# Edge-gated graph layer with residual layer norm: the first 16 parts' edges in one tile, head work queued behind table chunks, two more gather buffers, other batch sizes at the end

## The chip, the cores and the metric

The kernel runs on one core of a Trainium2 chip. A core has five engines that run their own instruction streams and wait for each other through semaphores: TensorE (PE, matrix products and transposes; PEld is its weight load), VectorE (DVE), ScalarE (ACT, activations and copies), GpSimd (POOL, which here only issues gathers) and SyncE (SP, which here issues transfers). The metric is device time in microseconds from start to end of one execution; lower is better.

## The reference

There are N = 12500 nodes with 128 features and E = 412500 directed edges (200000 edges in both directions and one loop for each node), sorted by destination.

```
theta = x[dst] - x[src]
w     = sigmoid(relu(theta @ W1 + b1) @ W2 + b2)      # one number for each edge
agg   = segment_sum(w * theta, dst)
indeg = segment_sum(1, dst)
out   = layernorm(x + agg + indeg * (x @ W4 + b4))
```

Since theta is a difference, theta @ W1 is y[dst] - y[src] with y = x @ W1, and the sum of w * theta over a node's edges is x times the sum of w, less the sum of w * x[src].

## The kernel before, in words

**Parts and blocks.** The edges are cut into 403 parts of 1024 (K = 8 groups of 128; the last part has 7 groups). Two parts make a block (202 blocks). As edges are sorted by destination, the destinations of a block lie in a window of WB = 96 consecutive nodes that begins at the block's first destination, and those of a part within 41.

**Head (lines 107 to 313).** The source and destination of the first 16 parts (`FIRST = 16`) are loaded with a part to a partition, 16 partitions of 1024 numbers; `turn` (L280) converts them to float on ACT (L283) and transposes them on PE (L288), 4 groups at a time; `place_src` (L294) writes the row numbers `src_i`, which the gathers use, and `place_dst` (L300 to L312) writes destinations relative to the part (`off`) and to the window (`rel`), and notes their largest and smallest values in `bad` (a check that they fit). `base_r` is each part's first destination, 403 separate numbers (L120); from it come `base_b`, `first_c`, `base_c`, `far` and `step_c` (L231 to L251), the broadcast over partitions being a matmul (L238). Lines 137 to 204 make constants: one-hot helpers, a split of b1 in three bf16 terms, and so on. The tile framework orders the instructions of each engine; only SP's order is that of the program (`manual_schedule`, L314).

**Table.** `table_chunk` (L333) computes z = [y, x] for all nodes, 12 chunks of 1024 rows and two small ones: the rows of x come in by a transfer issued from ACT (L329), PE transposes four groups of 128 rows into the PSUM tile `pw` (L342), ACT copies them to `txT` (L344), PE multiplies by W1 into `ph` (L346); when both halves are through, DVE copies y (L348) and ACT copies x (L349) into a buffer `zt`, and SP writes it to z in HBM (L350). There are three `zt` buffers and one `pw`.

**Gathers.** `gather(s)` (L224) issues a part's K indirect transfers from POOL, each fetching 128 rows. The first NH = 8 parts fetch rows of x (so that they need not wait for z), and the later parts rows of z. There are NZ = 8 buffers `zbuf`; parts 0 to 7 take half a buffer each (zbuf 0 to 3), zbuf 4 to 6 are also the table's `zt`, and part 8 onwards goes round all of them from zbuf 4. A buffer can be filled again when its part's ACT work (L456) has read it. POOL issues in the order of the parts, and each gather waits for the landing of the one 8 before.

**Main loop (L552 to L574).** Step s issues the gather of part s + 4, the block's window (y of the 96 nodes and its spread, L360 to L386), the one-hots of part s + 2 (`one_hot`, L389), the spread of y to edges (`spread_y`, L400, PE), and `weights(s)` (L434): DVE subtracts the gathered y (L448), takes relu times W2 (L449) and sums to logits (L453); ACT makes the sigmoid (L454) and scales the gathered x rows (L456, 8 for each part). For the first 8 parts `both` (L418) computes the product with W1 on PE, as no y was gathered. `one_hot_w(s - 1)` (L409, a 128x768 compare) and `add_up(s - 2)` (L459) follow: PE sums the part's rows into the window (L474), 16 matmul instructions.

**End of a block (`total`, L487 to L524).** First up to one finished row block is stored (two in the last nine blocks), then the sums are copied (L494), PE computes x @ W4 + b4 in `pu` (L497, L498), DVE and ACT combine the terms (L505 to L509) and take mean and variance (L512, L513). The inverse root is taken for LB = 8 blocks together (L518, L519), as ACT has to switch its table between sigmoid and square root; the last three blocks close their batch at once. `store` (L480) makes `o` on DVE (L484) and SP writes it (L485); `o` has 4 buffers. At the very end the flag from `bad` is read (L580 to L586); were it set, a slow general version would run.

Of the kernel before, what the change touches and what calls it, by code (L numbers as in the profile page):

```python
# [28 lines left out]
NZ = 8  # L29
AHEAD = 4  # L30
LB = 8
NH = 8
FIRST = 16
# [4 lines left out]
def gnn_resnorm(  # L38
# [76 lines left out]


    loaded = [load(nc.sync, src, *sets[0])]
    base_r = const.tile([1, NS], I32, name="base_r")
    with nc.allow_non_contiguous_dma(reason="each part's first dst"):
        nc.sync.dma_start(  # L120
            base_r, bass.AP(tensor=dst.tensor, offset=dst.offset, ap=[[0, 1], [BE, NS]]))
    wts = const.tile([P, 2, D], F32, name="wts")
    nc.sync.dma_start(wts[:, 0, :], W1)
    loaded.append(load(nc.sync, dst, *sets[0]))
# [13 lines left out]
    nc.vector.tensor_copy(ident_b, ident)  # L138
# [10 lines left out]
    nc.vector.tensor_scalar_mul(wneg, wts[:, 0, :], -1.0)  # L149
# [7 lines left out]
    nc.scalar.activation(fix[:, :WB], iota_row[:, :WB], AF.Copy)  # L157
    nc.scalar.activation(fix[:, P:2 * P], w2_r, AF.Copy)
    iota_f = fix[:, :WB].rearrange("p (o m) -> p o m", o=1)
    w2_f = fix[:, P:2 * P].rearrange("p (o m) -> p o m", o=1)  # L160


    def at_least(name, n, v=1.0):
        c = const.tile([P, 1], F32, name=name)
        nc.vector.tensor_scalar(c, iota_p, float(n), v, op0=OP.is_ge, op1=OP.mult)
        return c

    ge = [at_least(f"ge{i}", i * SW) for i in range(4)]
    eb = [at_least(f"eb{i}", 3 * SW + i) for i in range(1, 4)]
    m12 = const.tile([P, 1], F32, name="m12")  # L170
    nc.vector.tensor_sub(m12, ge[3], ge[1])
    m2 = const.tile([P, 1], F32, name="m2")
    nc.vector.tensor_sub(m2, ge[3], ge[2])
    one_c = const.tile([P, 1], F32, name="one_c")
    nc.vector.tensor_sub(one_c, ge[3], eb[2])
    place_c = const.tile([P, 1], F32, name="place_c")
    nc.vector.tensor_add(place_c, ge[1], ge[2])
    nc.vector.tensor_scalar(place_c, place_c, -float(SW), None, op0=OP.mult)
    nc.vector.tensor_add(place_c, place_c, iota_p)
    nc.vector.scalar_tensor_tensor(place_c, ge[3], -4.0 * N, place_c, op0=OP.mult, op1=OP.add)  # L180

    YB = WB + 3
    yb_buf = [const.tile([P, D], F32, name=f"yb{i}") for i in range(2)]
    bh = const.tile([P, D], BF16, name="bh")
    b1_s = const.tile([P, D], F32, name="b1_s")
    e_c = const.tile([P, 1], F32, name="e_c")
    nc.vector.memset(b1_s, 0.0)
    for i in range(3):
        nc.vector.tensor_copy(bh, b1_r)
        nc.vector.tensor_scalar(e_c, iota_p, float(WB + i), None, op0=OP.is_equal)  # L190
        nc.vector.scalar_tensor_tensor(b1_s, bh, e_c, b1_s, op0=OP.mult, op1=OP.add)
        nc.vector.tensor_sub(b1_r, b1_r, bh)
    for t in yb_buf:
        nc.vector.tensor_copy(t[WB:, :], b1_s[WB:, :])


    behind = const.tile([P, P], F32, name="behind")
    nc.vector.memset(behind, -4.0)
    for i in range(3):
        nc.vector.tensor_copy(behind[:WB, i * SW:(i + 1) * SW], lag[:WB, :SW])  # L200
    own = behind[WB:, 3 * SW:3 * SW + 3]
    nc.vector.tensor_scalar(own, lag[WB:, 3 * SW:3 * SW + 3], float(WB - 3 * SW), 4.25,
                            op0=OP.is_equal, op1=OP.mult)
    nc.vector.tensor_scalar(own, own, -4.0, None, op0=OP.add)
# [27 lines left out]
    nc.vector.tensor_scalar(base_b, base_r[:, ::SUB], float(N - WB), None, op0=OP.min)  # L232
    base_f = const.tile([1, NS], F32, name="base_f")
    nc.vector.tensor_copy(base_f, base_r)
    first_c = const.tile([P, NS], F32, name="first_c")
    with tc.tile_pool(name="pre_ps", bufs=1, space=bass.MemoryType.PSUM) as pps:
        pb = pps.tile([P, NS], F32, name="pb")
        nc.tensor.matmul(pb, ones_r, base_f, start=True, stop=True)  # L238
        nc.vector.tensor_copy(first_c, pb)
    base_c = const.tile([P, NK, SUB], F32, name="base_c")  # L240
    for h in range(SUB):
        nc.vector.tensor_scalar(base_c[:, :, h], first_c[:, ::SUB], float(N - WB), None,
                                op0=OP.min)
    nc.vector.tensor_scalar(first_c, first_c, float(N - SW), None, op0=OP.min)
    base_cs = base_c.rearrange("p b h -> p (b h)")
    far = const.tile([P, NS], F32, name="far")
    nc.vector.tensor_sub(far, first_c, base_cs[:, :NS])
    nc.vector.memset(far[WB:, :], 0.25)
    step_c = const.tile([P, NK], F32, name="step_c")
    nc.vector.tensor_sub(step_c[:, 1:], base_c[:, 1:, 0], base_c[:, :NK - 1, 0])  # L250
# [4 lines left out]
    nc.vector.tensor_copy(bad[:, 0:1], base_c[:, 0:1, 0])  # L255
    nc.vector.tensor_scalar(bad[:, 1:2], base_c[:, NK - 1:, 0], -1.0, float(N - WB),
                            op0=OP.mult, op1=OP.add)
    nc.vector.tensor_reduce(bad[:, 2:3], step_c, AX.X, OP.max)
    nc.vector.tensor_scalar(bad[:, 2:3], bad[:, 2:3], -float(WB), None, op0=OP.add)
    nc.vector.tensor_reduce(bad[:, 3:4], step_c, AX.X, OP.min)  # L260
    nc.vector.tensor_scalar(bad[:, 3:4], bad[:, 3:4], -1.0, None, op0=OP.mult)
# [51 lines left out]

    with tc.manual_schedule(engines={SP}), tc.tile_pool(name="work", bufs=2) as wp, tc.tile_pool(  # L314
# [11 lines left out]
        def table_load(c):  # L326
            n0, np_, m = chunks[c]
            xt = tp.tile([P, TC, D], F32, name="xt", bufs=4)
            nc.scalar.dma_start(  # L329
                xt[:np_, :m, :], x[n0:n0 + np_ * m, :].rearrange("(p t) d -> p t d", t=m))  # L330
            return xt

        def table_chunk(c, xt):  # L333

            n0, np_, m = chunks[c]
            zt = zbuf[NX + c % 3]
            py = ps_h.tile([P, K, D], F32, name="ph")
            for g0 in range(0, m, G):
                g = min(G, m - g0)
                px = ps_l.tile([P, G, P], F32, name="pw")  # L340
                for j in range(g):
                    nc.tensor.transpose(px[:, j, :np_], xt[:np_, g0 + j, :], ident[:np_, :np_])  # L342
                xT = tp.tile([P, G, P], F32, name="txT")
                nc.scalar.activation(xT[:, :g, :np_], px[:, :g, :np_], AF.Copy)  # L344
                for j in range(g):
                    nc.tensor.matmul(py[:np_, g0 + j, :], xT[:, j, :np_], wts[:, 0, :],  # L346
                                     start=True, stop=True)
            nc.vector.tensor_copy(zt[:np_, :m, :D], py[:np_, :m, :])  # L348
            nc.scalar.activation(zt[:np_, :m, D:], xt[:np_, :m, :], AF.Copy)  # L349
            nc.sync.dma_start(  # L350
                z[n0:n0 + np_ * m, :].rearrange("(p t) d -> p t d", t=m), zt[:np_, :m, :])

# [56 lines left out]
        def one_hot_w(s):  # L409

            n = tiles(s)
            ow = wp.tile([P, K, WB], F32, name="ow", bufs=3)
# [46 lines left out]
        def add_up(s):  # L459
# [12 lines left out]
            end = h == SUB - 1 or s == NS - 1  # L472
            for k in range(n):
# [6 lines left out]
        def store(n):  # L480
            for _ in range(min(n, len(ready))):
                base, vb, mean, rstd = ready.pop(0)
                o = wp.tile([P, D], F32, name="o", bufs=4)
                nc.vector.tensor_scalar(o[:WB], vb, mean, rstd, op0=OP.subtract, op1=OP.mult)  # L484
                nc.sync.dma_start(out[ds(base, WB), :], o[:WB])  # L485

        def total(b):  # L487
            d = blocks.pop(b)
            pa = d["pa"]
            left = NK - 1 - b  # L490

            store(1 if left > 8 else 2)
            a = wp.tile([P, AW], F32, name="a")
            nc.scalar.activation(a[:WB], pa[:WB], AF.Copy)  # L494
            carry[0] = a
            pu = ps_l.tile([P, G, P], F32, name="pw")[:, 0, :]
            nc.tensor.matmul(pu[:WB], ones_r[:, :WB], b4_r[0:1, :], start=True, stop=False)  # L497
            nc.tensor.matmul(pu[:WB], d["xwT"][:, :WB], wts[:, 1, :], start=False, stop=True)  # L498
            if not batch:
# [4 lines left out]
            sw = wp.tile([P, 1], F32, name="sw")  # L504
            nc.scalar.activation(sw[:WB], a[:WB, D:D + 1], AF.Copy, bias=1.0)  # L505
            own = fix[:WB, (2 + b % 2) * P:(3 + b % 2) * P]
            nc.scalar.activation(own, d["xw"][:WB], AF.Copy, scale=sw[:WB])
            nc.vector.tensor_sub(v[:WB, i, :], own, a[:WB, :D])
            nc.vector.scalar_tensor_tensor(  # L509
                v[:WB, i, :], pu[:WB], a[:WB, D + 1:], v[:WB, i, :], op0=OP.mult, op1=OP.add)  # L510
# [4 lines left out]
            if len(of) == LB or left < 3:  # L515
# [7 lines left out]
            if left < 3:  # L523
                store(len(ready))  # L524
# [4 lines left out]

        fetch(0)  # L530
        fetch(1)
        xts = [table_load(0), table_load(1)]
        place_src(0, ps_l, loaded[0])
        for s in range(AHEAD):
            gather(s)
        place_dst(0, ps_l, loaded[1])
        for c in range(len(chunks)):
            if c + 2 < len(chunks):
                xts.append(table_load(c + 2))
            table_chunk(c, xts.pop(0))  # L540
# [7 lines left out]
        window(0)  # L548
        one_hot(0)
        spread_y(0)  # L550
        one_hot(1)
        for s in range(NS + 2):  # L552
# [14 lines left out]
            if s < NS:  # L567
                weights(s)
            if s + 2 < NS:
                one_hot(s + 2)  # L570
            if 0 < s <= NS:
                one_hot_w(s - 1)
# [197 lines left out]
```

## Time and profile before

| what | value |
|---|---|
| median of 3 runs | 4102.65 us (4101.36 to 4108.0) |
| the profiled execution, its time | 4108.91 us |
| its span, first to last instruction | 4107.1 us |
| busy: POOL, DVE, PE, ACT | 3053.3, 2589.6, 2435.7, 1589.9 us |
| first gather starts | 12.09 us |
| first gather from z starts | 98.77 us |
| last gather ends | 4071.37 us |
| last output store is issued | 4101.5 us |

Times in the profile's lines are microseconds from the first instruction; a timeline line gives the start, the duration, the engine (with a q where only the engine's sequencer works, as for issuing transfers), the line of the kernel, the operation, what is written and read, how many instructions stand together, and in brackets the idle time of the engine before it with what ended it. A group's line in the page gives the total busy time, the mean duration in ns, and the idle time before. "PEclk" is the share of TensorE's full clock that was granted. The profile is of one execution.

### The profile page before, as it was taken

The numbers are of one execution on the slowest core, as the hardware profiler recorded it, in microseconds if no ns is written. First come the engines' busy times: TensorE is split into PE (matmuls) and PEld (weight loads), VectorE is DVE, ScalarE is ACT, GpSimd is POOL, SyncE is SP. The second block draws the span as 40 slices with busy tenths as digits, with TensorE's granted clock in tenths as the row PEclk, the third lists the DMA queues.
The fourth block names the chain that finished last, engine by engine and source line by source line (L and its number), as shares of the span: only waits on it lengthen the run. The fifth ranks groups of instructions, "written<-read, shape, count | busy, mean of one in ns | idle before, by whom it ended". The sixth has DMA issues, their size and how long they took to land.

```text
span 4107.1 us, 52566 instructions
## 1 busy us (share of the span) xinstructions
PE 2435.7 (59%) x16083; PEld 2124.1 (52%) x16083; DVE 2589.6 (63%) x4254; ACT 1589.9 (39%) x5206; POOL 3053.3 (74%) x3232
## 2 busy tenths in 40 slices
PE   5766555565555566566556555555555555556554
PEld 4655545455445455555555555454555555545544
DVE  3587676666666666676666666666666666666665
ACT  3454344333333333343433433333334334333332
POOL 6677777777777777777777777777777777777774
PEclk8877666666766666666666666666666666666666
DMA  7333433333333333343333333333333333333332
GB/s 247 88 110 111 121 110 110 110 110 110 111 110 110 110 110 111 115 115 110 111 111 111 110 111 110 110 112 110 110 112 110 110 110 111 111 110 110 110 112 78
DMA packets 205395, 464.62 MB, mean 113 GB/s; under 512 B 59264, under 2 KB 99112, under 8 KB 203566
## 3 DMA queue, kind: packets, MB, share of 16 engines
q0 software_dynamic: 153680, 418.46, 35.7%
q1 hardware_dynamic: 49452, 36.31, 2.9%
q10 hardware_dynamic: 1970, 6.40, 0.4%
q8 instruction: 128, 2.10, 0.2%
q14 instruction: 165, 1.35, 0.1%
HBM read 438.21 MB, written 22.73 MB: 112 GB/s over the span
## 4 chain that ended last, share of the span: by engine, by line
DVE 33%; DMA 25%; PE 22%; ACT 14%; issue 5%; POOL 0%; DVEq 0%; ACTq 0%; SPq 0%; POOLq 0%
DMA zbuf<-z,src_i 24%; DVE h L448 9%; PE pa L474 9%; ACT wx L456 8%; DVE h L449 6%; DVE lg L453 5%; DVE oh L396 5%; PE pw L378 4%; DVE ow L413 3%; ACT yh L380 1%; PE ph L406 1%; ACT wx L454 1%; PE pw L368 1%; PE pd L394 1%; PE pa L470 1%
## 5 line engine op out<-in xcount | busy, mean ns | idle before, releaser
L226 POOL DMA_INDIRECT zbuf<-z,src_i x3159 | 2991.1, 947 | 988.0 <-issue 445.6
L448 DVE TENSOR_TENSOR h<-ph,zbuf 128x1024 f32<-128x1024 f32 x395 | 483.4, 1224 | 1181.7 <-DMA zbuf<-z,src_i 1181.4
L474 PE MATMUL pa<-wx,ow 128*96 128x130 f32 x6446 | 1127.9, 350 | 2.8 <-DVE ow L413 1.5
L474 PEld LDWEIGHTS pa<-wx,ow 128*96 128x96 f32 x6446 | 1092.0, 227 | 4.7 <-DVE ow L413 2.0
L456 ACT ACTIVATE wx<-zbuf,wx 128x128 f32<-128x128 f32 x3223 | 1005.0, 389 | 9.2
L394 PE MATMUL pd<-ident_b,off 128*128 128x128 bf16 x3223 | 338.4, 261 | 805.5 <-DVE oh L396 800.1
L394 PEld LDWEIGHTS <-off 128*128 128x128 bf16 x3223 | 269.9, 118 | 616.8 <-issue 604.4
L453 DVE TENSOR_REDUCE lg<-h 128x8 f32<-128x1024 f32 x403 | 486.8, 1208 | 0.2
L449 DVE SCALAR_TENSOR_TENSOR h<-h,fix 128x1024 f32<-128x1024 f32 x395 | 477.5, 1209 | 0.0
L494 ACT ACTIVATE a<-pa 96x130 f32<-96x130 f32 x202 | 55.5, 275 | 1012.9 <-PE pa L474 1012.9
L406 PE MATMUL ph<-y,oh 128*128 128x128 bf16 x3159 | 295.8, 247 | 200.9 <-DVE y L385 189.5
L413 DVE TENSOR_TENSOR ow<-fix,rel 128x768 f32<-128x768 f32 x403 | 380.6, 945 | 0.0
L406 PEld LDWEIGHTS <-oh 128*128 128x128 bf16 x3159 | 259.2, 114 | 232.5 <-issue 210.2
L396 DVE TENSOR_SCALAR oh<-pd,place_c,one_c 128x1024 bf16<-128x1024 bf16 x403 | 320.7, 796 | 42.8 <-PE ph L430 34.6
L378 PEld LDWEIGHTS pw<-yb,pick 99*128 99x128 f32 x806 | 184.3, 317 | 301.8 <-issue 224.6
L366 ACT ACTIVATE xwT<-pw 128x96 f32<-128x96 f32 x202 | 48.3, 239 | 564.0 <-PE pw L364 563.9
L378 PE MATMUL pw<-yb,pick 99*128 99x128 f32 x806 | 236.6, 447 | 39.5 <-ACT yb L370 39.3
L380 ACT ACTIVATE yh<-pw 128x256 bf16<-128x256 f32 x202 | 77.2, 382 | 428.7 <-PE pw L378 428.6
L368 PE MATMUL pw<-wts,xwT 128*96 128x128 f32 x404 | 130.2, 419 | 185.3 <-ACT xwT L366 185.0
L470 PE MATMUL pa<-a,sh 96*96 96x130 f32 x402 | 140.6, 453 | 143.1 <-DVE sh L468 141.7
L381 DVE SCALAR_TENSOR_TENSOR pw<-yh,m,pw 128x256 f32<-128x256 bf16 x202 | 98.5, 488 | 178.2 <-ACT yh L380 176.9
L364 PE MATMUL pw<-ident,xw 96*128 96x96 f32 x202 | 72.4, 359 | 207.2 <-DVE v L509 200.4
(113 smaller groups left out, 1930.1 us busy)
## 6 DMA issues: line engine op xcount, KB each, us to landing
zbuf<-z,src_i POOLq DMA_INDIRECT x3159, 2.8
z<-zbuf SPq DMA_DIRECT2D x12, 1024.0 KB
xw<-in_x_dram SPq DMA_DIRECT2D x202, 48.0 KB
out_dram<-o SPq DMA_DIRECT2D x202, 48.0 KB
xt<-in_x_dram ACTq DMA_DIRECT2D x12, 512.0 KB
zbuf<-in_x_dram,src_i POOLq DMA_INDIRECT x64, 4.2
e_i<-in_src_dram SPq DMA_DIRECT2D x2, 512.0 KB
e_i<-in_dst_dram SPq DMA_DIRECT2D x2, 512.0 KB
```

The lines of the kernel that those rows point to most:

```text
L226: nc.gpsimd.indirect_dma_start(out=rows_of(s)[:, k, :], out_offset=None, in_=z if s >= NH else x, in_offset=IndirectOffsetOnAxis(ap=src_i[ ...
L378: nc.tensor.matmul(py[:, h, :], pick[:YB], yb[:YB], start=True, stop=True)
L394: nc.tensor.transpose(pd[:, k, :], off[:, k, s:s + 1].to_broadcast([P, P]), ident_b)
L396: nc.vector.tensor_scalar(oh[:, :n, :], pd[:, :n, :], place_c, one_c, op0=OP.is_equal, op1=OP.max)
L406: nc.tensor.matmul(d["ph"][:, k, :], d["oh"][:, k, :], blocks[b]["y3"][:, h, :], start=True, stop=True)
L413: nc.vector.tensor_tensor(ow[:, :n, :], iota_f.to_broadcast([P, n, WB]), rel[:, :n, s:s + 1].to_broadcast([P, n, WB]), op=OP.is_equal)
L448: nc.vector.tensor_sub(h[:, :n, :], d["ph"][:, :n, :], zs[:, :n, :D])
L449: nc.vector.scalar_tensor_tensor(h[:, :n, :], h[:, :n, :], 0.0, w2_f.to_broadcast([P, n, D]), op0=OP.max, op1=OP.mult)
L453: nc.vector.tensor_reduce(lg[:, :n], h[:, :n, :], AX.X, OP.add)
L456: nc.scalar.activation(wx[:, k, :D], xs[:, k, :], AF.Copy, scale=wx[:, k, D:D + 1])
L470: nc.tensor.matmul(bd["pa"][:WB], sh[:WB, :WB], carry[0][:WB], start=True, stop=False)
L474: nc.tensor.matmul(bd["pa"][:WB], d["ow"][:, k, :], wx_buf[s % 3][:, k, :], start=h == 0 and k == 0 and carry[0] is None, stop=end and k = ...
```

## The change: what it does

- **First edges.** The first 16 parts' indices are loaded as one tile of 128 partitions with 128 numbers each (a partition holds one group), so that one conversion, one transpose and one copy replace two transposing rounds. Source and destination tiles have the same name in a pool with one buffer.
- **Bases in two pieces.** The first destinations of parts 0 to 15 are loaded apart from the other 387; `bases` is called for each piece, `check_bases` after the second.
- **Order at the head.** Chunks 0 and 1 of the table are written first; first bases, first destinations and constants are queued behind those chunks (`after` makes an instruction follow given ones on their engines); the long bases behind chunk 7, the first window and one-hots behind chunk 9. The table's loads use zbuf 7 and 8 instead of tiles of their own, and its transposes go into `pw` and `pd` in turn.
- **Buffers.** NZ is 10 instead of 8; `ow` has 4 buffers instead of 3; LB is 6 instead of 8.
- **Order in the loop.** `one_hot_w(s)` stands ahead of `weights(s)` (before: `one_hot_w(s - 1)` after the one-hots of s + 2). `pu` is computed ahead of the block's last sums.
- **End.** The last 12 blocks close their batch at 2 blocks, the last two at 1, and up to three blocks are stored at each of the last 12; stores come at the end of `total` instead of its beginning.

```
-NZ = 8
+NZ = 10
-LB = 8
+LB = 6
-FIRST = 16
+FIRST = P // K
...
+    def load_first(edges):
+        t = const.tile([P, P], I32, name="f_i")
+        nc.sync.dma_start(t, edges[:P * P].rearrange("(p e) -> p e", e=P))
+        return t
+    src_f = load_first(src)
...
+    load_bases(0, FIRST)
     wts = const.tile([P, 2, D], F32, name="wts")
     nc.sync.dma_start(wts[:, 0, :], W1)
-    loaded.append(load(nc.sync, dst, *sets[0]))
+    dst_f = load_first(dst)
+    load_bases(FIRST, NS)
...
+    def first_turned(t, ps):
+        f = ep.tile([P, P], F32, name="f_f")
+        nc.scalar.activation(f, t, AF.Copy)
+        pt = ps.tile([P, G, P], F32, name="pw")[:, 0, :]
+        nc.tensor.transpose(pt, f, ident)
+        return pt.rearrange("p (s k) -> p k s", k=K)
+    def place_first_src(ps):
+        nc.scalar.activation(src_i[:, :, :FIRST], first_turned(src_f, ps), AF.Copy)
...
         def table_load(c):
-            xt = tp.tile([P, TC, D], F32, name="xt", bufs=4)
+            h = c % 4
+            xt = zbuf[NX + 3 + h // 2].rearrange("p k d -> p (k d)")
...
-                px = ps_l.tile([P, G, P], F32, name="pw")
+                px = ps_l.tile([P, G, P], F32, name="pd" if g0 else "pw")
...
+            if end:
+                bd["pu"] = ps_l.tile([P, G, P], F32, name="pw")[:, 0, :]
...
-            if len(of) == LB or left < 3:
+            if len(of) == LB or (left < 12 and len(of) == 2) or left < 2:
...
-            if left < 3:
-                store(len(ready))
+            for _ in range(min(1 if left >= 12 else 3, len(ready))):
...
+        place_first_src(ps_l)
+        for s in range(AHEAD):
+            gather(s)
+        chunk()
+        chunk()
+        with after(done[0]):
+            bases(0, FIRST, ps_l)
+        with after(done[1]):
+            place_first_dst(ps_l)
+            place_c, one_c, m12, m2, yb_buf, behind = constants()
         fetch(0)
         fetch(1)
...
+        while len(done) < len(chunks):
+            chunk()
+        with after(done[7]):
+            bases(FIRST, NS, ps_l)
+            check_bases()
...
+        with after(done[9]):
+            window(0)
+            one_hot(0)
+            spread_y(0)
+            one_hot(1)
...
             if s < NS:
+                one_hot_w(s)
                 weights(s)
             if s + 2 < NS:
                 one_hot(s + 2)
-            if 0 < s <= NS:
-                one_hot_w(s - 1)
```

## The prediction

> **What bounds the kernel now.** I read the busy table first, then windows of the span, then the waits of GpSimd (POOL), then the timelines of the first 210 us and of the last 40 us.
>
> The page's busy table and one of its groups:
>
> ```profile
> PE 2435.7 (59%) x16083; PEld 2124.1 (52%) x16083; DVE 2589.6 (63%) x4254; ACT 1589.9 (39%) x5206; POOL 3053.3 (74%) x3232
> ...
> L226 POOL DMA_INDIRECT zbuf<-z,src_i x3159 | 2991.1, 947 | 988.0 <-issue 445.6
> ```
>
> No engine is full, but POOL does one thing: it issues 64 + 3159 = 3223 gathers, 947 ns each. Two equal windows (span, then PE, PEld, DVE, ACT, POOL, clock, DMA share, GB/s):
>
> ```profile
> 800.00:1600.00 800.00, 469.38 (x3088) 410.44 (x3088) 505.25 (x806) 304.88 (x1015) 605.16 (x640) 0.68 0.39 110
> 2400.00:3200.00 800.00, 465.59 (x3094) 406.15 (x3094) 509.27 (x850) 306.99 (x1019) 605.35 (x640) 0.68 0.39 111
> ```
>
> 640 gathers per 800 us in both: one per 1.25 us, 0.95 of work and 0.30 between two. DVE needs 506 of those 800 us, PE 470. So the middle is set by POOL's issue rate, and an edit there that is not on POOL moves nothing. What can move is where POOL does not issue. POOL's timeline has five such places (idle time before each, in brackets):
>
> ```profile
> 12.09 1.19 POOL L226 DMA_INDIRECT zbuf<-in_x_dram,src_i  x1 [10.33 <-ACT fix L158]
> 91.34 0.95 POOL L226 DMA_INDIRECT zbuf<-in_x_dram,src_i  x1 [0.30 <-issue]
> 98.77 0.94 POOL L226 DMA_INDIRECT zbuf<-z,src_i  x1 [6.48 <-DVE pick L375]
> 164.78 0.95 POOL L226 DMA_INDIRECT zbuf<-z,src_i  x1 [1.31 <-PE pw L378]
> 180.91 0.94 POOL L226 DMA_INDIRECT zbuf<-z,src_i  x1 [11.43 <-ACT wx L456]
> 198.36 0.94 POOL L226 DMA_INDIRECT zbuf<-z,src_i  x1 [7.76 <-ACT wx L456]
> 4070.42 0.95 POOL L226 DMA_INDIRECT zbuf<-z,src_i  x1 [0.30 <-ACT wx L456]
> ```
>
> The account: 12.09 us to the first gather; 64 gathers at 1.2485 to 92.29; 6.18 beyond the usual 0.30 until table z has landed (98.77; the releaser named, a DVE one-hot, is only what came last; the wait is for all z writes); 1.01 + 11.13 + 7.46 = 19.6 us for buffers at parts 14.5, 15 and 16; the rest at (4070.42 - 98.77 - 19.6) / 3158 = 1.2514; then 35.7 us from the last gather's end at 4071.37 to 4107.1. The buffers: parts 12 to 15 go into zbuf 0 to 3, which hold the x rows of parts 0 to 7, and ACT finished those at 187.3 (part 7) and 200.1 (part 8, zbuf 4).
>
> **The change, part by part.** Times are of the profiled execution (4108.91 us, span 4107.1).
>
> *First gather.* Before, the source indices wait for PE, where the transposes stand behind a matmul on all 403 first destinations:
>
> ```profile
> 8.89 0.26 DVE L232 TENSOR_SCALAR base_b<-base_r 1x202 int32<-1x202 int32 x1 [7.43 <-DMA base_r<-in_dst_dram]
> 9.48 1.71 PE L238 MATMUL pb<-base_f,ones_r 1*128 1x403 f32 x2 [9.48 <-DVE base_f L234]
> 11.58 0.23 ACT L294 ACTIVATE src_i<-pw 128x64 int32<-128x64 f32 x1 [5.97 <-PE pw L288]
> ```
>
> After, one tile, one transpose and one copy come first on PE. But on ACT the order is: copy of the indices (from 3.46, after the table load; 128x128, about 0.28), the issue of table load 2 (it waits for W1), the copy of chunk 0 (1.04), the issue of load 3 (it waits for load 1), and only then src_i. Loads 0 and 1, 1 MB, had arrived by 6.0 in the trace's packets; W1 should land around 6, no longer behind 403 four-byte packets. So src_i ends near 7.1, gather 0 starts at 7.5 (6 to 10). With 64 x 1.2485, POOL is ready for z at 87.4.
>
> *Table.* Its order on PE, ACT and DVE now puts chunks 0 and 1 ahead of destinations and constants. The dst tile uses the same buffer as the src tile and is issued last on SP, behind the long base list (landed at 8.87 before; say 9.5), so it lands near 12; ACT holds its copy ahead of chunk 0's first txT. So: txT 12.3, matmuls at half clock to 16.3, copy 1.22, z write 0 at 17.8 (29.3 before) and 1 at 21.5. Then DVE has about 40 small operations (first bases, checks, constants; some 8 us by their durations before) ahead of chunk 2's copy, and four `ow` (0.94 each) and two `sh` before chunk 5's: writes 2, 3, 4 near 30.4, 33.8, 36.8. Write 2 stood at 38.7 before, so it is two chunks ahead. Seven full chunks and two small ones remain. Compute: one half-chunk at full and at half clock:
>
> ```profile
> 59.66 1.06 PE L342 MATMUL pw<-ident,xt 128*128 128x128 f32 x4
> 61.47 2.07 PE L346 MATMUL ph<-wts,txT 128*128 128x128 f32 x8 [0.75 <-ACT txT L344]
> 65.14 1.16 PE L346 MATMUL ph<-wts,txT 128*128 128x128 f32 x8 [0.75 <-ACT txT L344]
> 66.13 0.60 PE L342 MATMUL pw<-ident,xt 128*128 128x128 f32 x4
> ```
>
> A chunk is 2 x (0.60 + 1.16) = 3.5 us or 2 x (1.06 + 2.07) = 6.3; the second PSUM buffer (pw, pd in turn) removes the 0.75 waits, which made it 4.7 and 7.35 before. The Trainium skill ("TensorE: Matmul & The Clock Gate", Part 1) says an idle stretch of about 3.4 us halves the clock and a busy window of that length restores it. The trace has the loss (idle 39.9 to 43.75, clock 0.5 from 44.5) but not the quick return: it stayed at 0.5 until 65. By the rule seven chunks take 25 us, by the row, half of them slow, 34. Transfer: from 30 us there remain 10.8 MB of z, 3.7 MB of x and 0.052 MB/us of gathers; at 320 to 360 GB/s (the best stretches showed 311 over 20 us, 360 over 5) this takes 47 to 54 us. That is the larger: done at 77 to 84, plus the 5 us that the last landing took before: 82 to 89. POOL is ready at 87.4, so the gather from z starts at 88.0, the middle of what both leave: 10.8 us earlier. The cover is thin: each us that the table is later than 87.4 comes straight off.
>
> *Ten buffers instead of eight.* Part p's gather now needs what part p - 10 read; parts 14 to 17 use zbuf 0 to 3. With z at 88.0 and 10.0 us a part: part 17's second half asks for part 7 at 183, part 18 for part 8 at 188. The main loop starts earlier: last chunk's copy near 77 to 80 instead of 92.1, minus 3.5 us for the long bases, which DVE does just there: 12 us earlier. So parts 7 and 8 end near 175 and 188. Stall left: 0.5 of 19.6, that is -19.1 (bounds 0 and 10 left).
>
> *One-hots ahead of logits, `pu` ahead of the sums.* Same instructions, other places. DVE has 3.7 us to spare per part; nothing on the path. The smaller batches make 38 square-root groups instead of 27, with two table loads of 1.28 us in most: some 28 us of ACT, hidden in its 61% idle time.
>
> *Tail.* Before, ten stores stand at the end, each waiting for a free `o` or a semaphore:
>
> ```profile
> 4077.44 1.28 ACT L518 ACT_TABLE_LOAD   x1
> ...
> 4079.69 22.11 SPq L485 DMA_DIRECT2D out_dram<-o  x10
> ```
>
> Now four are left; the last (block 201) is bound by compute. Relative to the same last gather (landed 4073.4): DVE's order puts h of part 402 ahead of the reduction for 401, so that is 2 us of late work more: lg(401) at 4075.8 (69.2 before), wx(401) to 78.6, sum of block 200 at 79.7, then ACT switches to square root for blocks 198/199 (1.28 + 0.3), back to sigmoid (1.28 + 0.3), 0.2 + 7 wx (2.14) to 85.2, own 0.37, switch 1.28, root of 200 to 87.1; PE's last matmul waits for `pu`, which waits for v(200) on DVE, to 87.4; copy, sw, own to 88.4; four DVE operations to 89.4; root, reciprocal, o to 90.2. The last store is issued at 4090.3, not 4101.5: -11.2. Here a rule speaks against the change: "ScalarE: Activation LUTs" (What ACT_TABLE_LOAD costs) gives a switch 2.66 us with its drain. The trace has 1.28 and the next activation 0.01 later (4077.44, then 4078.73), so I take the row; by the page three switches would cost 4.1 more, leaving -7.
>
> **Sum.** -10.8 - 19.1 - 11.2 = -41.1: 4108.91 becomes 4067.8. That execution was 6.3 above the median of the runs, 4102.65, so the forecast is 4061.5 us.
>
> **Rivals.** (1) The table stays late: the DVE constants ahead of chunk 2, or a half-clock stretch, push z's landing to 97. The head gives 2 instead of 10.8: 4070. For it: two engines in one order, 0.6 us of slack. Against: even at half clock PE needs 44 us for the seven chunks and has 50. (2) The buffers' stall only moves: if the main loop starts no earlier (long bases, DVE at 95% from 200 us on), parts 7 and 8 end at 187 and 200 against 183 and 188, 12 us come back: 4074. (3) Slower: gathers themselves become dearer, by any new contention of POOL's descriptor work. Price 3223 x the added time; from 12.8 ns a gather (1%) the gain is gone, from 15.3 it is slower by 0.2%; at 30 ns the time is 4158. For it: the first two gathers took 1.19 us, beside a busy start. Against: from the 400th gather on, means over each 400 lie between 1.2510 and 1.2523 us apart, whatever stood beside them. (4) The change doesn't do what it says: gather 0 stays at 12 since src_i waits behind ACT's loads, and the tail's switches cost the page's price: 4072 to 4077.
>
> **Numbers.** 0.2% (8.2 us) is about what a measurement of this kernel can tell from no change. The sum as worked, within 10 us: 0.70; rival 1: 0.10; rival 2: 0.08; rival 4: 0.06 (all faster); no difference 0.02; rival 3: 0.04. Faster 0.94, same 0.02, slower 0.04. Range: table (5 either way), stall (to 10), tail (4), execution spread (3): 4048 to 4080.
>
> **What would show it.** First gather near 7.5, first z gather near 88; no idle time over 2 us on POOL after it; last gather ending near 4042; some 24 us from there to the end, four stores at the last. Wrong if gathers are not 1.25 us apart, if the wait before the first z gather is over 4 us, or if wx lines again release gathers around parts 17 and 18.

## The result: some seven tenths of the gain that was forecast

| | kernel before | changed kernel |
|---|---|---|
| median of 6 runs | 4106.1 us (4101.36 to 4109.25) | 4076.39 us (4075.43 to 4077.38) |
| profiled execution, its span | 4108.91, 4107.06 us | 4076.45, 4074.68 us |

The ratio is 0.9929 (95% interval 0.9916 to 0.9942). The forecast was 4061.5 us with a range of 4048 to 4080: the direction and the range hold, and the gain is smaller than forecast (29.7 us instead of some 41). Ratios below are to the kernel before on the same chip.

The changed kernel's page, busy table and costliest group:

```profile
PE 2401.4 (59%) x16071; PEld 2090.6 (51%) x16071; DVE 2572.8 (63%) x4264; ACT 1657.5 (41%) x5239; POOL 3056.6 (75%) x3232
...
L241 POOL DMA_INDIRECT zbuf<-z,src_i x3159 | 2994.7, 948 | 962.2 <-issue 546.2
```

Two windows of its middle and two of its end (span, then PE, PEld, DVE, ACT, POOL, clock, DMA share, GB/s):

```profile
800.00:1600.00 800.00, 458.95 (x3079) 399.87 (x3079) 498.80 (x800) 313.83 (x1014) 605.44 (x639) 0.67 0.39 110
2400.00:3200.00 800.00, 454.77 (x3080) 395.72 (x3080) 503.56 (x850) 320.21 (x1026) 605.55 (x639) 0.67 0.39 111
4047.00:4052.00 5.00, 0.00 (x0) 0.00 (x0) 2.78 (x5) 0.50 (x2) 0.03 (x1) 0.63 0.13 30
4052.00:4057.00 5.00, 4.74 (x20) 4.18 (x20) 3.23 (x7) 2.26 (x8) 0.00 (x0) 0.50 0.00 0
```

The middle is what it was, 639 gathers in 800 us. The end differs: 5 us without a matmul, then 5 us at a granted clock of 0.50. POOL's timeline (first gather, first gather from z, last gather):

```profile
10.11 1.10 POOL L241 DMA_INDIRECT zbuf<-in_x_dram,src_i  x1 [8.35 <-ACT src_i L345]
...
90.35 0.95 POOL L241 DMA_INDIRECT zbuf<-z,src_i  x1 [0.30 <-issue]
...
4046.09 0.95 POOL L241 DMA_INDIRECT zbuf<-z,src_i  x1 [0.30 <-issue]
```

After the first gather POOL never waits again: not one idle time above 0.35 us among 3222. Four terms make up the difference of the two spans, each read from the two POOL timelines. The pitch is the time from one gather's start to the next; the tail is what follows the last gather's end:

| term | forecast | measured | how |
|---|---|---|---|
| head, to the first gather from z | -10.8 | -8.4 | 98.77 to 90.35 |
| waits for buffers | -19.1 | -19.6 | all gone |
| pitch of the other 3158 gathers | 0 | +3.7 | 1.25145 to 1.25261 us |
| tail, last gather's end to the end | -11.2 | -8.0 | 35.69 to 27.65 |
| sum | -41.1 | -32.4 | |

The buffers' term is tested alone below (f3, f2). Those of the head and the tail are read from the traces: no run undoes just the edits behind them.

### The profile page after: what moved, and what is told of

It is laid out like the page before. It is cut to its first block, busy times and chain, and to the rows that moved or that the text cites. A ratio compares the mean times of both kernels' runs of the same rounds, so it can differ in the third digit from the quotient of the medians.

```text
span 4074.7 us, 52688 instructions
## 1 busy us (share of the span) xinstructions
PE 2401.4 (59%) x16071; PEld 2090.6 (51%) x16071; DVE 2572.8 (63%) x4264; ACT 1657.5 (41%) x5239; POOL 3056.6 (75%) x3232
## 4 chain that ended last, share of the span: by engine, by line
DVE 34%; DMA 22%; ACT 19%; PE 18%; issue 6%; POOL 1%; DVEq 0%; SPq 0%; ACTq 0%; POOLq 0%
DMA zbuf<-z,src_i 21%; ACT wx L515 13%; DVE h L507 9%; PE pa L539 8%; DVE lg L512 8%; DVE h L508 7%; DVE oh L455 5%; ACT wx L513 2%; PE pw L437 2%; DVE pw L440 2%; PE ph L465 1%; PE pd L453 1%; PE pw L427 1%; PE pa L529 1%; POOL zbuf L241 1%
## 5 line engine op out<-in xcount | busy, mean ns | idle before, releaser
L539 PEld LDWEIGHTS pa<-wx,ow 128*96 128x96 f32 x6446 | 1075.3, 222 | 17.6 <-ACT wx L515 15.2
L515 ACT ACTIVATE wx<-zbuf,wx 128x128 f32<-128x128 f32 x3223 | 985.6, 388 | 11.0
L465 PE MATMUL ph<-y,oh 128*128 128x128 bf16 x3159 | 313.9, 246 | 231.2 <-DVE y L444 172.7
L423 PEld LDWEIGHTS pw<-ident,xw 96*128 96x128 f32 x202 | 32.6, 162 | 602.2 <-DVE v L560 596.8
L442 ACT ACTIVATE ym<-pw 128x256 bf16<-128x256 f32 x202 | 76.6, 379 | 421.1 <-DVE pw L440 421.1
L513 ACT ACTIVATE wx<-lg,b_c 128x8 f32<-128x8 f32 x403 | 123.3, 306 | 245.2 <-DVE lg L512 244.7
```

The lines of the kernel that those rows point to most:

```text
L465: nc.tensor.matmul(d["ph"][:, k, :], d["oh"][:, k, :], blocks[b]["y3"][:, h, :], start=True, stop=True)
L513: nc.scalar.activation(wx[:, :n, D], lg[:, :n], AF.Sigmoid, bias=b2_c)
L515: nc.scalar.activation(wx[:, k, :D], xs[:, k, :], AF.Copy, scale=wx[:, k, D:D + 1])
L539: nc.tensor.matmul(bd["pa"][:WB], d["ow"][:, k, :], wx_buf[s % 3][:, k, :], start=h == 0 and k == 0 and carry[0] is None, stop=end and k = ...
```

## Experiments

There are twelve runs of nine kernels, from three chips, and the chip decides what each can tell. The f runs are from a chip like that of the profiles (kernel before 4109.9 us). The e and the g runs are from two other chips, on each of which the kernel before takes 5141 us (5140.82 and 5140.66): there TensorE holds up the loop, and they answer a question that had not been asked. They are told last.

### Buffers without the head (f3), head without the buffers (f2)

f3 is the kernel before with the ten buffers; the table's loads go into zbuf 7 and 8, as there is no room for tiles of their own beside ten buffers.

```
-NZ = 8
+NZ = 10
...
-            xt = tp.tile([P, TC, D], F32, name="xt", bufs=4)
+            h = c % 4
+            xt = zbuf[NX + 3 + h // 2].rearrange("p k d -> p (k d)")
...
```

> The kernel before with the ten buffers alone, on a chip whose kernel before takes about 4103 us. Theory: 19.6 us of waits for buffers fall to about 1.3 us, first gather 12.1, first gather from z 98.8, tail 35.7: 18 us faster, 4088. Rival, the stall only moves: 7 us faster, 4099.

Measured: 4086.25 us (4083.95 to 4092.25), ratio 0.9950 (0.9933 to 0.9967). POOL's timeline, first gather, first from z, and the first of part 15 (which had waited 11.43 us):

```profile
11.89 1.20 POOL L226 DMA_INDIRECT zbuf<-in_x_dram,src_i  x1 [10.12 <-ACT fix L158]
...
96.02 0.94 POOL L226 DMA_INDIRECT zbuf<-z,src_i  x1 [3.92 <-DMA e_i<-in_src_dram]
...
166.02 0.95 POOL L226 DMA_INDIRECT zbuf<-z,src_i  x1 [0.30 <-ACT txT L429]
```

No wait is left at parts 14 to 18: 19.6 us gone, and the wait for z is 2.6 us shorter in this execution, so the span falls by 22.5 us (4107.06 to 4084.55). The rival "the stall only moves" falls.

f2 undoes the same in the changed kernel (NZ = 8, `xt` of their own).

> The changed kernel with NZ = 8 again and the table's loads in tiles of their own, on a chip whose kernel before takes about 4103 us. Theory: the earlier head already shrinks the stall; part 15 asks at 160.4 for part 6 (ACT until 164.3) and part 16 at 175 for part 8 (182.2): 12 us come back, 4088. If buffers and head simply add: 19.6 us come back, 4096. If the earlier main loop alone would have removed the stall: 4076.

Measured: 4086.33 us (4084.82 to 4089.30), ratio 0.9948 (0.9932 to 0.9965). POOL's timeline, the three places where it waits:

```profile
164.84 0.94 POOL L241 DMA_INDIRECT zbuf<-z,src_i  x1 [4.49 <-ACT wx L514]
...
170.29 0.94 POOL L241 DMA_INDIRECT zbuf<-z,src_i  x1 [0.75 <-PE pa L538]
...
182.62 0.95 POOL L241 DMA_INDIRECT zbuf<-z,src_i  x1 [7.64 <-ACT wx L514]
```

Beyond the usual 0.30 these are 12.0 us, where the theory had 12 (in the changed kernel ACT is through with part 6 at 164.3 and with part 8 at 182.2). The span is 10.25 us longer than the changed kernel's, as pitch and tail came out 2 us shorter in this execution; the medians differ by 9.9. In waits of POOL, buffers are worth 19.6 us with the old head and 12.0 with the new one. The new head lets the main loop run some 17 us earlier (part 7 done at 169.7 instead of 187.3) and so takes 7.6 of the stall away itself. The gains of the two edits overlap; only measured together, or with the times at which each buffer comes free, do they add to the right sum.

### Where the head's missing 2.4 us are (f1)

ACT's timeline in the changed kernel from the landing of the indices to the first gather's release (ACTq lines are the issuing of the table's loads):

```profile
5.22 0.31 ACT L339 ACTIVATE f_f<-f_i 128x128 f32<-128x128 int32 x1 [2.28 <-DMA f_i<-in_src_dram]
...
8.22 0.33 ACTq L379 DMA_DIRECT2D zbuf<-in_x_dram  x1
8.60 1.06 ACT L399 ACTIVATE zbuf<-zbuf 128x1024 f32<-128x1024 f32 x1 [3.07 <-DMA b_r<-in_L_gnn_b_dram]
...
9.56 0.27 ACT L345 ACTIVATE src_i<-pw 128x128 int32<-128x128 f32 x1
```

PE had the transposed indices ready at 6.13. ACT, in order, held their last copy until 9.56 behind a load's issue, which waited until 8.22, and a chunk's copy. f1 moves both conversions to DVE; it also makes the one-hot `pick` by another instruction, which is read elsewhere (the pitch).

```
-        nc.scalar.activation(f, t, AF.Copy)
+        nc.vector.tensor_copy(f, t)
...
-        nc.scalar.activation(src_i[:, :, :FIRST], first_turned(src_f, ps), AF.Copy)
+        nc.vector.tensor_copy(src_i[:, :, :FIRST], first_turned(src_f, ps))
...
-                nc.vector.tensor_scalar(pick[:YB], behind[:YB],
-                                        far[:YB, b * SUB + h:b * SUB + h + 1], None,
-                                        op0=OP.is_equal)
+                nc.vector.tensor_tensor(pick[:YB], behind[:YB],
+                                        far[:YB, j:j + 1].to_broadcast([YB, P]),
+                                        op=OP.is_equal)
```

> The changed kernel with two edits that are read at different places. (a) The conversion and the placing of the first 16 parts' indices go to DVE, which is idle there, in place of ACT, which issues a load and copies a chunk between the two: theory, first gather at 6.8 instead of 10.1 us, still no wait before the first gather from z (the table was complete at about 79, POOL asks at 87), so 3.3 us; rival, the table is delayed and POOL waits for it at 87: nothing. (b) The one-hot pick by a tensor_tensor compare: theory, gathers of over 975 ns go, mean pitch from the 400th gather on 1.2527 to 1.2510, 5 us; rival, they stay, 0 us. Both theories: 4068; both rivals: 4076.

Measured: 4076.36 us (4075.76 to 4083.85), ratio 0.9923 (0.9906 to 0.9939). The timeline of its head, and POOL's first gather from z:

```profile
5.20 0.23 DVE L339 CAST f_f<-f_i 128x128 f32<-128x128 int32 x1 [4.02 <-DMA f_i<-in_src_dram]
...
6.06 0.29 DVE L345 CAST src_i<-pw 128x128 int32<-128x128 f32 x1 [0.63 <-PE pw L341]
...
6.64 1.10 POOL L241 DMA_INDIRECT zbuf<-in_x_dram,src_i  x1 [4.88 <-DVE src_i L345]
...
87.78 0.94 POOL L241 DMA_INDIRECT zbuf<-z,src_i  x1 [0.30 <-issue]
```

The trace agrees with part (a): the first gather at 6.64 (6.8 expected), no wait at 87.78. So 3.5 us before the first gather lay in ACT's queue. Of these 2.6 are left at the first gather from z, as the 64 gathers before it stand 1.268 us apart here and 1.254 in the changed kernel. In the times no gain is seen: the other three executions took 4075.76 to 4076.88 us, the changed kernel's six 4075.43 to 4077.38. They have no trace, so where the 2.6 us went is open.

Part (b) falls: the gathers above 960 ns from the 400th on are 116 here, not fewer than the changed kernel's 101. The profiled execution took 4083.85 us, and its trace shows by what: the span is 7.2 us above that of the changed kernel, 9.9 from the pitch (1.25573 us) less 2.6 of the head and 0.1 of the tail. The usual gather took 949 ns instead of 946; the traces of e2 and g4 have 949 too, the other eleven 946.

### The place of `pu` in the tail (f4)

In the changed kernel the sums of block 200 were complete 2 us later after the last gather than I had worked out, with `pu`'s matmuls among them, waiting for `v` of the block before. f4 puts `pu` behind the sums again.

```
             end = h == SUB - 1 or s == NS - 1
-            if end:
-                bd["pu"] = ps_l.tile([P, G, P], F32, name="pw")[:, 0, :]
...
             for k in range(n):
                 nc.tensor.matmul(bd["pa"][:WB], d["ow"][:, k, :], wx_buf[s % 3][:, k, :],
...
+            if end:
+                bd["pu"] = ps_l.tile([P, G, P], F32, name="pw")[:, 0, :]
```

> The changed kernel with pu computed after the block's last sums again, on a chip whose kernel before takes about 4103 us. Theory: in the tail pu ahead of the sums holds TensorE for v of the block before, 2.0 us at block 200 and 0.9 at block 201; without it the tail from the last gather's end falls from 27.7 to about 24.8 us, time 4073.5. Rival: pu then lies on the path after the last sum: tail 27.7 to 29.2, time 4076.4 to 4078.

Measured: 4074.4 us (4073.68 to 4074.8), ratio 0.9918 (0.9901 to 0.9935); but the tail is 27.95 us, not 24.8. What it gained over 4076.39 lies in the pitch (1.25194 us from the 400th gather on, against 1.2527); all its four executions are below all six of the changed kernel, which was not run beside it. The tail of 24.8 that the theory promised did not come. The changed kernel's tail: first PE's rows of an earlier block, at the full clock (`pu`, then 16 sums), then all engines from the landing of the last gather:

```profile
4039.02 0.46 PE L534 MATMUL pw<-b_r,ones_r 1*96 1x128 f32 x2
4039.41 0.46 PE L536 MATMUL pw<-wts,xwT 128*96 128x128 f32 x2
4039.70 1.94 PE L539 MATMUL pa<-wx,ow 128*96 128x130 f32 x16
...
4049.22 1.09 DVE L507 TENSOR_TENSOR h<-ph,zbuf 128x896 f32<-128x896 f32 x1 [6.51 <-DMA zbuf<-z,src_i]
...
4052.26 0.75 PE L539 MATMUL pa<-wx,ow 128*96 128x130 f32 x2 [8.01 <-ACT wx L515]
...
4052.94 0.74 PE L534 MATMUL pw<-b_r,ones_r 1*96 1x128 f32 x2
...
4054.14 3.24 PE L539 MATMUL pa<-wx,ow 128*96 128x130 f32 x14
...
4057.42 0.28 ACT L548 ACTIVATE a<-pa 96x130 f32<-96x130 f32 x1 [3.16 <-PE pa L539]
4057.71 1.28 ACT L572 ACT_TABLE_LOAD   x1
...
4059.01 0.29 ACT L572 ACTIVATE sd<-mv,eps_c 96x2 f32<-96x2 f32 x1
```

and that of f4:

```profile
4049.86 2.91 PE L533 MATMUL pa<-wx,ow 128*96 128x130 f32 x12 [7.18 <-ACT wx L515]
...
4052.70 0.74 PE L538 MATMUL pw<-b_r,ones_r 1*96 1x128 f32 x2
...
4053.37 1.18 PE L533 MATMUL pa<-wx,ow 128*96 128x130 f32 x4
...
4054.59 0.28 ACT L548 ACTIVATE a<-pa 96x130 f32<-96x130 f32 x1 [2.73 <-PE pa L533]
...
4058.74 1.28 ACT L572 ACT_TABLE_LOAD   x1
...
4060.24 2.14 ACT L515 ACTIVATE wx<-zbuf,wx 128x128 f32<-128x128 f32 x7
```

`a` comes 10.39 us after the last gather's end in the changed kernel (4057.42 less 4047.03) and 9.94 in f4 (4054.59 less 4044.65): moving `pu` gave 0.45. It is not a clean test, for the order that came out still has half of a `pu` among the sums (L538, 0.74 us). Then f4 loses the gain: the last of three table switches, with its root (1.28 + 0.3), stands ahead of the last scalings on ACT, where the changed kernel has it behind them. In both, PE had stood idle for 7 to 8 us and then ran its sums at a granted clock of 0.5 (in f4 from 4045.2 to the end): the 14 matmuls of the changed kernel take 3.24 us, 0.23 each, where 16 at the full clock took 1.94.

### The chips on which TensorE holds up the loop (e1 to e4, g1 to g4)

On these two chips TensorE pauses between matmuls for 0.5 to 2 us at a time, while it waits for nothing that the profile shows. The sums' group in the stretch 1000 to 2000 us, first the changed kernel of the profiles above, then the same kernel on the third chip (g1):

```profile
L539 PE MATMUL pa<-wx,ow 128*96 128x130 f32 x1600 | 281.4, 349 | 0.0
```

```profile
L539 PE MATMUL pa<-wx,ow 128*96 128x130 f32 x1271 | 272.8, 362 | 215.7 <-issue 215.6
```

The mean of one is nearly the same; 215.6 us of pauses stand between them. Why TensorE pauses no run shows. What it does to the rest is seen in g1's timeline of one block:

```profile
1107.06 0.27 PE L539 MATMUL pa<-wx,ow 128*96 128x130 f32 x1 [1.34 <-issue]
...
1109.16 0.27 PE L539 MATMUL pa<-wx,ow 128*96 128x130 f32 x1 [1.83 <-issue]
...
1115.09 0.28 ACT L548 ACTIVATE a<-pa 96x130 f32<-96x130 f32 x1 [13.62 <-PE pa L539]
...
1115.93 0.29 ACT L513 ACTIVATE wx<-lg,b_c 128x8 f32<-128x8 f32 x1
...
1116.93 0.94 POOL L241 DMA_INDIRECT zbuf<-z,src_i  x1 [4.96 <-ACT wx L515]
```

The sums of a block end late, the copy `a` waits 13.6 us for them on ACT, the next part's sigmoid, whose logits were there at 1104.4, stands behind `a` in ACT's order, and so its buffer comes free late: POOL waits 5 us in this block and in the two beside it (209 waits in the whole run, for 202 blocks). The mean pitch there is 1.57 us.

The e runs are the same kernels as f3, f2 and f4, and the changed kernel with f1's `pick` alone (e4).

> The kernel before with the ten buffers alone (NZ = 10, the table's loads in zbuf 7 and 8 as in the changed kernel). Theory: the 19.6 us of waits for buffers fall to about 1.3 us (part 18 asks at 198.8 for the buffer of part 8, which ACT read until 200.1), first gather still at 12.1, first gather from z still at 98.8, tail still 35.7: about 18 us faster than before, 4088. Rival 'the stall only moves': 12 us come back at parts 17 and 18, about 7 us faster, 4099.

> The changed kernel with NZ = 8 again and the table's loads in tiles of their own. Theory: the earlier head already shrinks the stall; part 15 asks at 160.4 for part 6 (ACT until 164.3) and part 16 at 175 for part 8 (182.2): 12 us come back, 4088. If buffers and head simply add: 19.6 us come back, 4096. If the earlier main loop alone would have removed the stall: 4076, unchanged.

> The changed kernel with pu computed after the block's last sums again. Theory: in the tail pu ahead of the sums holds TensorE for v of the block before, 2.0 us at block 200 and 0.9 at block 201; without it the tail (last gather's end to the end) falls from 27.7 to about 24.8 us, time about 4073.5. Rival: the sums were late for another reason, and pu now lies on the path after the last sum (1.5 us): tail 27.7 to 29.2, time 4076.4 to 4078.

> The changed kernel with the one-hot pick made by a tensor_tensor compare with a broadcast operand in place of a tensor_scalar compare. Theory: the gathers of over 975 ns (each overlaps the beginning of a pick) go, the mean pitch from the 400th gather on falls from 1.2527 to about 1.2510 us, time falls by some 5 us to 4071. Rival: pick only happens to stand there, another cause makes these gathers long: pitch 1.2527, time 4076.

The g runs are the changed kernel unaltered (g1); with one rule of order for the last part on DVE (g2); with three edits (g3: the indices on DVE, the rule of g2 extended to the one-hot of part 402, the inverse root of the last four blocks as three and one); and with the old order of the weighted one-hot (g4).

```
g2, in weights(s); last holds the logit sum of the part before:
+                with after(last if s == NS - 1 else []):
                     nc.vector.tensor_sub(h[:, :n, :], d["ph"][:, :n, :], zs[:, :n, :D])
...
g3, besides:
-            if len(of) == LB or (left < 12 and len(of) == 2) or left < 2:
+            if len(of) == LB or (3 < left < 12 and len(of) == 2) or left < 2:
...
+                with after(last_wx if left < 2 else []):
                     nc.scalar.activation(sd[:WB, :m], mv[:WB, :m, 1], AF.Sqrt, bias=eps_c[:WB])
...
g4, in the main loop:
-                one_hot_w(s)
                 weights(s)
...
+            if 0 < s <= NS:
+                one_hot_w(s - 1)
```

> The changed kernel unaltered, for its pitch and tail beside the next three on one chip. If the 1 ns that the mean pitch rose by (1.2515 to 1.2525) belongs to the kernel: 1.2525 again, last gather's end at 4047. If it belongs to the execution: between 1.2513 and 1.2523, last gather's end at 4043 to 4046. Tail 27.6 either way.

> The changed kernel with one rule of order on DVE: the subtraction of the last part (402) stands behind the logit sum of part 401, which was ready 6 us before but stood behind it. Theory: this order, not pu, makes the tail long; the work of blocks 199 and 200 is done while the last gather is on its way; lg(402) at 6.8 us after the last gather's end instead of 8.0, then sigmoid, a table switch, 7 scalings: sums at 11.3, last store issued at 14.5, end at 20: tail 20 instead of 27.6, 7.6 us faster. Rival: the tail is bound by what follows lg(402) alone (TensorE and the table switches): 1.2 us faster.

> Three edits together: indices placed by DVE (first gather at 6.6 instead of 10.1, no wait for z at 87.8); the last part's subtraction behind lg(401) and behind the one-hot of part 402; the last four blocks' inverse root taken as three and one, behind the scalings of part 402, so that one table switch is left in the tail and stands beside TensorE's sums. Theory: head 3.4 us less, tail 18 us instead of 27.6: 13 us faster than the changed kernel. Rival 'tail bound by what follows': tail 25, 6 us faster.

> The changed kernel with the weighted one-hot of a part again behind its logits and the next part's one-hot (the order of the kernel before). Theory: the new order on DVE puts the two picks of a block beside the beginning of a gather more often; undone, the gathers of over 960 ns from the 400th on fall from 101 (8.2 us above the usual 945) to some 65 (4.6 us), 3 us faster. Rival: the number is a matter of the execution: no difference beyond what g1_after shows. Nothing else moves: no wait on POOL after the first gather.

| kernel | median us | ratio to the kernel before there (95%) |
|---|---|---|
| g1: changed | 5237.54 | 1.0187 (1.0173 to 1.0201) |
| e2: changed, NZ = 8 | 5228.07 | 1.0174 (1.0156 to 1.0191) |
| e4: changed, `pick` | 5241.51 | 1.0197 (1.0180 to 1.0214) |
| g2: changed, DVE rule | 5235.47 | 1.0181 (1.0167 to 1.0195) |
| g3: changed, three edits | 5240.06 | 1.0193 (1.0179 to 1.0207) |
| e1: before, NZ = 10 | 5158.2 | 1.0036 (1.0026 to 1.0046) |
| e3: changed, `pu` late | 5157.52 | 1.0033 (1.0019 to 1.0048) |
| g4: changed, one-hot order undone | 5091.37 | 0.9901 (0.9886 to 0.9916) |

None of these expectations is answered as it was meant: all were written for a POOL-bound loop with a tail of 28 us (36 for e1), and here POOL's longer idle times add up to 967 us after the 400th gather in g1 and the tail is 81 us (g2 82, g3 84). g3's first gather is at 6.72, as f1's, and buys nothing. So the theory of g2 and g3 (that DVE's order in the tail costs 7 to 10 us), and g4's of the long gathers, remain open, and no version is shown clear of the noise to beat the changed kernel where POOL is the bound.

What the table does show: where TensorE pauses, the changed kernel is 1.9% slower than the one before, the same change that gains 0.7% elsewhere. Two more buffers gain nothing there (e1 is 0.4% slower than its partner; e2, with two fewer, 0.2% faster than g1). The loop's order is what costs: the weighted one-hot ahead of the logits 146 us (5237.5 less 5091.4, 0.72 us a block), `pu` ahead of the sums 80 us (e3 against g1, from two chips whose kernels before agree within 0.2 us; 0.40 a block). No run undoes both. Both figures include what the framework's ordering of other instructions makes of the edit. With the one-hot's order undone, the rest of the change gains 1%.

## Why the prediction was right or wrong

**Bound.** Right: POOL's issue rate sets the middle in both kernels, 0.95 busy and 0.30 between, and the gain came only from places where POOL did not issue.

**First gather.** 7.5 (6 to 10) forecast, 10.11 measured. The step that failed is "src_i ends near 7.1". Two terms were too small: the indices landed at 5.22 and not at 3.46 (the row of before was for 16 partitions of 4 KB; 128 rows of 512 bytes came later), and the load's issue waited until 8.22, not 6. Only the second was on the path, as PE had the transposed indices ready at 6.13. I had named the queue that src_i stands in; f1 shows that it costs 3.5 us. The pitch of 1.2485 us that the forecast used for the first 64 gathers is also too small for its own row: from 12.09 to 92.59 (98.77 less the 6.18 of waiting) it is 1.258 in the kernel before. The changed kernel had 1.254, so this cost 0.3 us.

**Table.** The forecast had it complete at 82 to 89 and thin cover. Its compute steps were near: z writes at 18.8, 22.0, 32.4, 35.8, 38.9 against 17.8, 21.5, 30.4, 33.8, 36.8. The transfer term was mis-sized: I took 320 to 360 GB/s from the best stretches of before; the changed kernel moved 404 over 40 to 60 us, and the last of z's packets landed before 78. In before the full chunks' writes to z were issued 4.7 to 7.8 us apart, as the chunks became ready; so its best stretches were not the transfers' limit. z was never late for POOL: the first gather alone set 90.35 (10.11 plus 64 gathers at 1.254, with no wait added), and the head gave 8.4 instead of 10.8. Rival 1 falls. The granted clock between 20 and 80 us was 0.79 to 0.83, between the two cases that the forecast had weighed; nothing hung on it.

**Buffers.** Right: 0.5 left of 19.6 forecast, nothing left. The parts were done at 169.7 and 182.2, 5 to 6 us earlier than I had worked out, so there was room. f2 shows the mechanism: 12.0 us of waits with eight buffers, where the list of times gave 12.

**One-hots ahead of logits, `pu` ahead of sums.** "Nothing on the path" held, nearly, and only as long as the time to spare on the other engines covered it. First, the pitch rose by 1.16 ns, 3.7 us in all. From the 400th gather on, 65 gathers of before took over 960 ns and 101 of the changed kernel, 4.3 and 7.7 us above 945 (g4's expectation counted from 940): nearly the whole of it. Most are the same gather of a block, and 59 of the 65 and 94 of the 101 overlap a `pick` on DVE. That another compare leaves them (f1) speaks against the kind of instruction. That the new order on DVE makes them is argued: where POOL is the bound, their number is 94 to 116 in the four traces with the new order and 65 and 78 (f3) in the two with the old. But what they cost does not part as clearly, 5.5 us in f4 and 5.2 in f3, whose pitches from the 400th gather on are 0.16 ns apart (1.25194 and 1.25178); and g4, which undoes the order, was run where it can't be read. How much of the 3.7 us belongs to the kernel and how much to the execution stays open. The forecast's rival 3 has the right direction, at a tenth of its threshold of 12.8 ns. Second, the price of the two orders where nothing covers it, which the prediction did not name, is 146 and 80 us.

**Tail.** 24.5 forecast, 27.65 measured. lg(401) at 4.4 and its last scaling at 7.2 us after the last gather's end are as worked out. The step that failed is "sum of block 200 at 79.7", 8.3 us after: it was 10.35. I let the sums keep pace with ACT; after 8 us without work PE ran them at 0.23 us each, behind `pu`.

By an estimate from the changed kernel's rows, both the clock and `pu` were needed for the delay: at the full-clock times of the block shown above (0.68 us for `pu`, 1.70 for 14 sums), with `pu` starting at 4052.94 as it did, the sums would have ended 8.3 us after the last gather, as forecast; at half clock without `pu`'s matmuls, 8.9; measured 10.35. No run kept PE at the full clock, and f4 takes out only half of `pu`, so this split is worked out and not tested.

The prediction weighed a rule for the clock on the table, that of the Trainium skill, "TensorE: Matmul & The Clock Gate", Part 1 (about 3.4 us of idle time halve it), and did not apply it where its own chain had an idle PE. In the trace the clock fell to 0.5 at 4048.29, 4.0 us after the last matmul, and stayed there for 10.2 us; in f4 it fell 2.6 us after the last matmul. But half clock is nothing special here: from 400 to 4000 us the changed kernel ran at it for 66% of the time (its clock records hold 0.5 and 1.0 only) and fell to it 180 times, while PE stood idle for over 3.4 us only some 114 times. So idleness is not shown to be the cause. The kernel before gave the same warning: it too was at 0.5 after its last gather, from 4068.8 to 4082.5.

The table switches cost 1.28, with the next activation 0.02 later (4057.71, then 4059.01), three of them as forecast; the 2.66 of the Trainium skill, "ScalarE: Activation LUTs" (What ACT_TABLE_LOAD costs), is not seen, and rival 4 falls there.

**From the span to the median.** The forecast took 41.1 from a profiled execution and set it against a median of three runs that lay 6.3 below that execution. The changed kernel's profiled execution lies on its median (4076.45, 4076.39). So the miss of 14.9 us is 8.7 of the sum and 6.3 of this step. The right base was the execution itself: 4108.91 less 32.4 is 4076.5.

## What to carry to other kernels

When an engine that only issues sets the pace, list every place where it does not issue, with the time at which what it waits for comes free; edits that move the same list overlap (19.6 or 12.0 us for the same two buffers), so work them out together. An edit that costs nothing because another engine sets the pace should have its price without that cover beside it: the order of the weighted one-hot, 3.7 us at most here, cost 146 us (2.8%) where TensorE paused. And where a chain of matmuls is on the path, as in the tail, price them at the clock that the trace grants most of the time, here one half, and not at the full one.

## What was not expected of the hardware

The same program has two regimes on different chips: the kernel before takes 4106 to 4110 us, and 5141 us on two of them, with TensorE pausing between matmuls (215.6 us in 1000 in the sums of g1 alone). The mean granted clock is 0.63 to 0.64 there against 0.68 to 0.69, too little to make the difference alone. Single executions differ by the duration of a POOL gather: 3 ns more on each of 3223 is 9.7 us, the size of what f1's profiled execution lost in its pitch. And the transfers of the table's stretch, gathers included, reached 404 GB/s over 20 us.
